# A 4-output convolution form with pixels kept apart by four, and softmax sums spread by way of DRAM

## The chip, the core and the metric

The kernel runs on one core of one Trainium2 chip. The metric is the time of the kernel on the device, in microseconds. Everything is computed in fp32. TensorE (PE) multiplies, VectorE (DVE) and ScalarE (ACT) work on tiles of 128 partitions, GpSimd (POOL) and SyncE (SP) issue most DMAs. TensorE's results land in banks of [128, 512] fp32, of which the program has eight.

## What is computed

`x` has 4 images of 256 channels and 64x64 pixels. It goes through four layers. Each is added to its input, and each reads its input group-normalised (`_gn`).

```
x = x + L0(_gn(x))
# L0: xs = relu(group_norm(conv3x3(x)))
#     f = einsum('bnc,bcm->bnm', theta(xs), phi(xs));  attn = softmax(f, -1)    # 4096 x 4096 an image
#     y = einsum('bnm,bmc->bnc', attn, g(xs));  return group_norm(conv1x1(y)) * 0.1 + xs
x = x + L1(_gn(x))   # linear attention: 4 heads of 32, softmax of q and of k, rmsnorm before and after
x = x + L2(_gn(x))   # depthwise 3x3 and 1x1 convolutions, both kernels generated from the image
x = x + L3(_gn(x))   # 1x1 convolution, mixed from four experts
```

## The kernel before

Channels lie in two halves (`NH`) of 128 partitions; an image's half is 4096 elements a partition. `xp` holds the image with a border, `big` what a layer makes of it, `tpg` theta, phi and g. `tt` (L118) and `stt` (L121) stand for VectorE's two tensor operations, so many rows of the profile carry these two lines. Tiles `k4` (1024 elements) come from ten buffers, `k2` (512) from six, filters `u` from four.

**Attention.** `attend(b)` does 128 steps an image: 8 blocks of 512 queries (`q`) by 16 blocks of keys (`m`). A step issues the two logits matmuls of the next step (`pf`, L655), each followed by ScalarE's exp into `pr` (L656), then two matmuls of this step into `py` (L694). VectorE adds `pr` to `tot`. After the sixteenth step, `ended(q)` runs alongside the next steps, one part a step: `inv` is the sum of tot's halves (L663), `pss` a matmul with ones that puts each query's sum on all partitions (L667), `inv` its reciprocal (L669), `yt = py * inv`, the 1x1 convolution `ps_wy` (L678) and ScalarE's copies to `wt`. The counts beside them (`guard`) are for a test on the range of values.

**Interleaving.** All is issued in the program's order, engine by engine (`manual_schedule`). While image b attends, a `Chain` runs beside it: the rest of the layers of image b-1 (`tail`), then the convolution of image b+1 (`convolve`). Each `yield n` of the chain adds n times its rate to a credit, and each whole credit lets one attention step out. A lower yield or a lower rate puts more of the chain between two steps. `w.later(n, f)` runs f n steps on.

**Convolution.** It is done with Winograd tiles, 4 output rows of 6 input rows, and 2 output columns of 4 input columns. For each of six transformed rows, `down` makes `ra` from the normalised image; for each of four transformed columns, `across` makes `v` (one VectorE operation of 1024 elements); `products` (L403) does two matmuls of 512 columns for each half of the outputs, with filters loaded from DRAM; `joined` adds the products to even and odd columns, `joining` and `rows_joined` join the rows into `image`, a view of `big`. Image 0 (`convolve_first`) has nothing beside it and does part of its rows with plain 3x3 products. `filter_across` works the filters out at the start and stores them in DRAM. `normalise` does half on VectorE (L474) and half on ScalarE (L476). `normed_relu` (L492) does eight ScalarE operations of 1024 and after each a DMA that adds the result to a copy of x in DRAM.

**Tail.** Layer 1 has chunks `qkv` (L784), then `outputs`, `scaled`, `added` for eight chunks of 512 pixels: `ps_o` (four matmuls of 256 columns, L852), squares on ScalarE (L854), `zr` by VectorE (L856) and POOL (L210), `z` by VectorE, transposes `ps_zt` (L875), a scaled addition and statistics (L877). Layer 2 starts with `hidden` (`ps_h`, L929) beside eight ScalarE operations that write `xp` (L942). The last image's tail runs after all attention.

Of the kernel before, what the change touches and what calls it, by code (L numbers as in the profile page):

```python
# [34 lines left out]
TY, MY, TX, MX = 6, 4, 4, 2  # L35
IY, IX = HW // MY, HW // MX

# [53 lines left out]
def conv_preact_fast(ctx: ExitStack, tc: tile.TileContext, guard, x, wc, wtpg, ww, wqkv, wout, w1cat, wd2,  # L91
# [11 lines left out]
    def k4(name):  # L103
        return wk.tile([P, CH], F32, tag="k4", name=name, bufs=10)
# [3 lines left out]
    def k2(name):  # L108
        return wk.tile([P, 512], F32, tag="k2", name=name, bufs=6)
# [18 lines left out]
    big = cp.tile([P, NH, N], F32, name="big")  # L128
    tpg = cp.tile([P, 3, N], F32, name="tpg")
    ra = cp.tile([P, NH, IY, HW + 2], F32, name="ra")  # L130
    rt = cp.tile([P, NH, IY, HW], F32, name="rt")
# [24 lines left out]
    bigf = big.rearrange("p h n -> p (h n)")  # L156
# [79 lines left out]
    filters = tc.dram_tile([TY, NH, P, TX, NH, P], F32, name="filters")  # L236
# [30 lines left out]
    def filter_across(a, stay=False):  # L267
# [4 lines left out]
        if stay:  # L272
            both = [k2("both_u").rearrange("p (h o) -> p h o", h=NH) for _ in range(2)]
        else:
            t = k4("both_u").rearrange("p (b h o) -> p b h o", b=2, h=NH)
            both = [t[:, b] for b in range(2)]
# [8 lines left out]
        for oh in range(NH):  # L285
            for k in range(TX):
                nc.sync.dma_start(out=filters[a, oh, :, k], in_=of(k)[:, :, bass.ts(oh, P)])
        return lambda k, oh, h: of(k)[:, h, bass.ts(oh, P)]

# [60 lines left out]
    def rows_of(k, h=None):  # L350

        sel = slice(k, k + MY * (IY - 1) + 1, MY)
        return xp[:, :, sel, :] if h is None else xp[:, h, sel, :]
# [4 lines left out]
    def down(a, to, prior=None):  # L358

        A, T = inside(to), rt  # L360
        mul, add, sub = ALU.mult, ALU.add, ALU.subtract
        if a in (0, 5):
# [9 lines left out]
        return [(stt, A[:, h], T[:, h], -2.0 if a == 2 else -4.0, inside(prior)[:, h], mul, add) for h in range(NH)]  # L372

    def across(k, rows):

        def col(j):
            return rows[:, :, :, j:j + MX * (IX - 1) + 1:MX]
# [3 lines left out]
        tt(v.rearrange("p (h y x) -> p h y x", h=NH, x=IX), col(first), col(second), op)  # L381
        return v

    ACROSS = (1, 2, 0, 3)

    def joiner(st):

        dst, one = [None] * NH, [None] * NH

        def stats(k):  # L390
            for oh in range(NH):
                for s in range(2):
                    nc.vector.bn_stats(st[:, oh, 2 * k + s, :], image[:, oh, bass.ts(s, IY // 2), k, :])
# [1392 lines left out]
```

## Time and profile before

| | |
|---|---|
| median of three runs | 3144.88 us (3144.27 to 3146.38) |
| profiled execution | 3145.76 us, its span 3144.0 us |
| granted TensorE clock, mean | 0.987 |
| VectorE, ScalarE, GpSimd busy | 66%, 36%, 4% of the span |
| chain that ended last | PE 80%, DVE 12%, issue 5%, ACT 2% |
| bytes read and written in HBM | 103.40 and 73.40 MB |

A group's row reads: line, engine, operation, output and inputs, shapes, count, then busy time in all and mean ns of one, then the engine's idle time just before and what ended it. An fp32 matmul appears as two records; records overlap, so what matmuls cost is read from where the next begins. In a timeline, the first number is the start and the second the length; what stands in brackets is the idle time before it.

```profile
PE   6899999999999999999999999999999999996888
DVE  8736766443547995877536896778363768855485
ACT  2233224332555332323364432222445443333510
```

These are the busy tenths of 40 equal slices: VectorE is densest where a convolution or layer 2's depthwise part runs beside attention.

### The profile page before, as it was taken

To read this page: it belongs to the slowest core of one execution; us is meant where nothing else is said; L and a number is where in the kernel's file an instruction comes from. 1 tells how busy PE (TensorE), PEld (TensorE's weight loads), DVE (VectorE), ACT (ScalarE), POOL (GpSimd) and SP (SyncE) were. 2 spreads that over 40 slices of the span, in tenths; PEclk is the share of its full clock that TensorE was granted. 3 is DMA by queue.
4 is the path that set the end of the run, shared out by engine and by line. 5 is a ranking of instruction groups with operands and counts; after the bars stand their busy time and mean duration, and the time that the engine had idled before them with its cause. 6 is when DMAs were issued, how large, how long until landed. Compare 5 with 4: busy or idle time off the path is not lost.

```text
span 3144.0 us, 24213 instructions
## 1 busy us (share of the span) xinstructions
PE 3033.0 (96%) x8526; PEld 1472.9 (47%) x8526; DVE 2079.6 (66%) x2611; ACT 1129.2 (36%) x2097; POOL 131.6 (4%) x175
## 2 busy tenths in 40 slices
PE   6899999999999999999999999999999999996888
PEld 3454444445564444444565444444545544443533
DVE  8736766443547995877536896778363768855485
ACT  2233224332555332323364432222445443333510
POOL 0000000000010000000011000000100100000100
PEclk9999999999999999999999999999999999998999
DMA  5610013001100023113300102310410010120011
GB/s 184 182 34 26 32 35 66 7 14 47 67 11 21 20 74 116 39 39 67 114 8 3 41 20 77 110 44 31 113 62 1 11 34 14 47 74 34 14 60 65
DMA packets 73985, 161.68 MB, mean 51 GB/s; under 512 B 7936, under 2 KB 39424, under 8 KB 70912
## 3 DMA queue, kind: packets, MB, share of 16 engines
q1 hardware_dynamic: 69248, 143.27, 13.3%
q0 software_dynamic: 4608, 16.78, 2.9%
q8 instruction: 70, 1.15, 0.2%
q14 instruction: 59, 0.48, 0.0%
HBM read 103.40 MB, written 73.40 MB: 56 GB/s over the span
## 4 chain that ended last, share of the span: by engine, by line
PE 80%; DVE 12%; issue 5%; ACT 2%; DMA 0%; POOL 0%; SPq 0%; POOLq 0%; ACTq 0%
PE pf L655 23%; PE py L694 23%; PE ps_conv L403 8%; PE ps_qkv L784 5%; DVE dw L121 4%; PE ps_tp L631 4%; PE ps_ex L1117 3%; PE ps_pw L979 3%; DVE tot L118 2%; PE ps_g L636 2%; PE ps_wy L678 2%; PE ps_o L852 1%; PE ps_ctx L806 1%; PE ps_dw L1014 1%; PE ps_ss L770 1%
## 5 line engine op out<-in xcount | busy, mean ns | idle before, releaser
L656 ACT ACTIVATE pr<-pf 128x512 f32<-128x512 f32 x1024 | 604.2, 596 | 1227.3 <-PE pf L655 1214.2
L655 PE MATMUL pf<-tpg 128*128 128x512 f32 x2048 | 967.2, 595 | 1.4 <-ACT pr L656 1.4
L694 PE MATMUL py<-pr,tpg 128*128 128x512 f32 x2048 | 962.1, 592 | 3.0 <-ACT pr L656 2.9
L118 DVE TENSOR_TENSOR tot<-tot,pr 128x1024 f32<-128x1024 f32 x448 | 546.3, 1219 | 249.7 <-ACT pr L656 248.1
L694 PEld LDWEIGHTS py<-pr,tpg 128*128 128x128 f32 x2048 | 388.8, 190 | 494.3 <-issue 479.8
L655 PEld LDWEIGHTS pf<-tpg 128*128 128x128 f32 x2048 | 381.5, 190 | 443.0 <-issue 419.1
L121 DVE SCALAR_TENSOR_TENSOR dw<-xp,dk,dw 128x1008 f32<-128x1008 f32 x216 | 272.9, 1267 | 6.8 <-ACT dw L971 3.7
L403 PE MATMUL ps_conv<-v,u 128*128 128x512 f32 x576 | 259.0, 596 | 3.6 <-DVE v L118 3.6
L403 PEld LDWEIGHTS ps_conv<-v,u 128*128 128x128 f32 x576 | 109.7, 191 | 143.5 <-issue 136.6
L784 PE MATMUL ps_qkv<-wqkv_s,xg 128*128 128x384 f32 x384 | 129.9, 487 | 0.0
L631 PE MATMUL ps_tp<-big,wtpg_s 128*128 128x512 f32 x256 | 118.0, 605 | 3.0 <-ACT big L492 3.0
L118 DVE TENSOR_TENSOR tpg<-ps_g,bg_s 128x512 f32<-128x512 f32 x32 | 22.1, 691 | 145.6 <-PE ps_g L636 145.6
L210 POOL TENSOR_TENSOR rstd<-rstd,half 128x2 f32<-128x2 f32 x24 | 16.8, 700 | 2419.3 <-DVE rstd L315 2225.7
L979 PE MATMUL ps_pw<-dw,pk 128*128 128x512 f32 x224 | 104.6, 601 | 8.1 <-DVE dw L121 8.1
L669 DVE RECIPROCAL inv<-pss 128x512 f32<-128x512 f32 x32 | 107.3, 3352 | 7.2 <-PE pss L667 7.2
L784 PEld LDWEIGHTS ps_qkv<-wqkv_s,xg 128*128 128x128 f32 x384 | 72.2, 190 | 53.6 <-issue 9.6
L794 DVE TENSOR_REDUCE qs<-qk 128x16 f32<-128x512 f32 x24 | 16.5, 686 | 119.0 <-ACT qk L788 119.0
L118 DVE TENSOR_TENSOR v<-ra 128x1024 f32<-128x1024 f32 x72 | 86.7, 1219 | 0.4
L632 ACT ACTIVATE tpg<-ps_tp,btp_s 128x512 f32<-128x512 f32 x64 | 43.9, 687 | 119.6 <-PE ps_tp L631 119.6
L631 PEld LDWEIGHTS ps_tp<-big,wtpg_s 128*128 128x128 f32 x256 | 47.9, 195 | 55.0 <-issue 50.6
L854 ACT ACTIVATE junk<-ps_o 128x256 f32<-128x256 f32 x128 | 49.2, 384 | 67.5 <-PE ps_o L852 59.4
L979 PEld LDWEIGHTS ps_pw<-dw,pk 128*128 128x128 f32 x224 | 43.0, 192 | 62.6 <-issue 51.9
(281 smaller groups left out, 2904.6 us busy)
## 6 DMA issues: line engine op xcount, KB each, us to landing
u<-filters SPq DMA_DIRECT2D x144, 128.0 KB, 2.3
xp<-in_x_dram SPq DMA_DIRECT2D x16, 1024.0 KB, 6.3
xs_d<-big POOLq DMA_DIRECT2D x32, 512.0 KB, 11.7
wy_d<-wt SPq DMA_DIRECT2D x32, 512.0 KB, 3.0
out_dram<-res SPq DMA_DIRECT2D x64, 256.0 KB, 2.0
wy<-wy_d SPq DMA_DIRECT2D x28, 512.0 KB, 5.2
xs<-xs_d SPq DMA_DIRECT2D x24, 512.0 KB, 5.3
wp<-in_wp_dram SPq DMA_DIRECT2D x16, 512.0 KB, 4.6
```

What stands on the lines that cost most here:

```text
L118: nc.vector.tensor_tensor(o, a, b, op)
L121: nc.vector.scalar_tensor_tensor(o, a, s, b, op0, op1)
L403: nc.tensor.matmul(ps[oh], u(oh, h), v[:, bass.ts(h, 512)], start=(h == 0), stop=(h == NH - 1))
L631: nc.tensor.matmul(ps, wtpg_s[:, h, k, :], big[:, h, cols], start=(h == 0), stop=(h == NH - 1))
L636: nc.tensor.matmul(ps[:, j, :], big[:, h, bass.ts(4 * c + j, P)], wtpg_s[:, h, 2, :], start=(h == 0), stop=(h == NH - 1))
L655: nc.tensor.matmul(pf, phi[:, bass.ts(2 * m + s, P)], theta[:, bass.ts(q, 512)], start=True, stop=True)
L656: nc.scalar.activation(pr[:, bass.ts(s, 512)], pf, AF.Exp)
L669: nc.vector.reciprocal(inv, pss)
L694: nc.tensor.matmul(py, g[:, bass.ts(2 * m + s, P)], probs[i][:, bass.ts(s, 512)], start=(m == 0 and s == 0), stop=(m == NM - 1 and s == 1))
L784: nc.tensor.matmul(ps[:, 0:3 * HID], xg[:, h, bass.ts(j, P)], wqkv_s[:, h, :], start=(h == 0), stop=(h == NH - 1))
L979: nc.tensor.matmul(ps, pk[:, h * NH * P + oh * P:h * NH * P + (oh + 1) * P], dw[h][:, bass.ts(s, 512)], start=(h == 0), stop=(h == NH - 1))
L1117: nc.tensor.matmul(ps, wm[h][:, bass.ts(oh, P)], big[:, h, cols], start=(h == 0), stop=(h == NH - 1))
```

## The change

Images 1 to 3 are convolved with 6 transformed columns that give 4 output columns, as the rows already did; image 0 keeps the old form, under names that end in `_first`. The normalised image is written into `big`, rearranged so that pixels 0, 4, 8 ... of a row stand side by side, then 1, 5, 9 ... and so on, each of the four runs with one pixel of border: rows of 68 elements (`planar`). `ra` and `rt` have such rows too, and the outputs lie in `outs`, a view of `xp`, in the same manner, as 16-element runs. Six columns are done as three pairs. `across` fills a `v` of two columns with four, three or four operations, `products` does eight matmuls of 256 columns into two banks, and `joined` makes sums and differences of a pair (`parts`), which are put into the four output columns when the second pair is there. `normed_relu` brings the pixels back in order in 16 ScalarE operations of 512 elements, and adds to DRAM in four pieces of 1 MB instead of eight of 512 KB. `normalise` puts six of its eight operations on ScalarE; it also clears the borders on GpSimd.

The filters of these images are made during the attention of image 0 (`filters_across`), from rows stored in DRAM (`rows_d`); at the start, only image 0's own are made. A load of filters is 256 KB, into three buffers in place of four of 128 KB. `k4` has nine buffers, `k2` five.

For 31 of the 32 blocks of queries, `ended` lets four matmuls with one column of ones put the sums on partitions, [128, 4], takes 512 reciprocals there, writes them to DRAM (`inv_d`) and reads them back to all partitions; two more steps of attention pass before `yt`.

Yields fall: `qkv` 0.125 to 0.04, layer 1's chunks before it 0.5 to 0.2, `outputs` twice 0.6 to twice 0.2, `hidden` 0.5 to 0.15, the mixing of experts 0.5 to 0.25. The rate for image 0's attention falls from 1.5 to 1.34; for images 1 and 2 it is 0.83 in the tail and 0.7 in the convolution instead of 0.86, and for image 3's attention 1.46 instead of 1.24.

```diff
-TY, MY, TX, MX = 6, 4, 4, 2
+TY, MY, TX, MX = 6, 4, 6, 4
 IY, IX = HW // MY, HW // MX
+TX1, MX1 = 4, 2
+IX1 = HW // MX1
+RW = MX * (IX + 1)
...
-        return wk.tile([P, CH], F32, tag="k4", name=name, bufs=10)
+        return wk.tile([P, CH], F32, tag="k4", name=name, bufs=9)
...
-        return wk.tile([P, 512], F32, tag="k2", name=name, bufs=6)
+        return wk.tile([P, 512], F32, tag="k2", name=name, bufs=5)
+    def filter_tile(name):
+        return wk.tile([P, NH, NH * P], F32, tag="u", name=name, bufs=3)
...
-    big = cp.tile([P, NH, N], F32, name="big")
+    big_all = cp.tile([P, NH, (HW + 2) * RW], F32, name="big")
+    big = big_all[:, :, 0:N]
     tpg = cp.tile([P, 3, N], F32, name="tpg")
-    ra = cp.tile([P, NH, IY, HW + 2], F32, name="ra")
-    rt = cp.tile([P, NH, IY, HW], F32, name="rt")
+    ra = cp.tile([P, NH, IY, RW], F32, name="ra")
+    rt = cp.tile([P, NH, IY, RW], F32, name="rt")
...
+    rows_d = tc.dram_tile([TY, P, NH, 3, NH * P], F32, name="rows_d")
+    filters = tc.dram_tile([TY, P, TX - 2, NH, NH * P], F32, name="filters")
...
+    def keep(rows):
+        for a in rows:
+            nc.sync.dma_start(out=rows_d[a], in_=u1[:, a].rearrange("p h (j o) -> p h j o", j=3))
...
+    def filters_across(w):
+        n = NH * 3 * NH * P
+        def load(a):
+            t = big[:, a % 2, 0:n].rearrange("p (h j o) -> p h j o", h=NH, j=3)
+            nc.sync.dma_start(out=t, in_=rows_d[a])
+            return t
+        loaded = [load(0), load(1)]
+        yield 2
+        for a in range(TY):
+            t = loaded[a]
+            f = big[:, a % 2, n:n + (TX - 2) * NH * NH * P].rearrange("p (k h o) -> p k h o", k=TX - 2, h=NH)
+            first, mid, last = (t[:, :, j, :] for j in range(3))
+            for op, *args in ((tt, f[:, 0], first, last, ALU.add), (tt, f[:, 1], f[:, 0], mid, ALU.subtract),
+                              (tt, f[:, 0], f[:, 0], mid, ALU.add), (stt, f[:, 2], last, 4.0, first, ALU.mult, ALU.add),
+                              (stt, f[:, 3], mid, -2.0, f[:, 2], ALU.mult, ALU.add),
+                              (stt, f[:, 2], mid, 2.0, f[:, 2], ALU.mult, ALU.add)):
+                op(*args)
+                yield 0.3
+            if a + 2 < TY:
+                loaded.append(load(a + 2))
+            nc.sync.dma_start(out=filters[a], in_=f)
...
+    planar = big_all.rearrange("p h (y x) -> p h y x", x=RW)
+    PIXEL = (50, 0, 17, 34, 51, 1)
+    outs = x_cols.rearrange("p h (j k n) -> p h k j n", j=MX, k=MY)
+    rt_outs = rt.rearrange("p h y x -> p h (y x)")[:, :, 0:N // MY].rearrange("p h (j n) -> p h j n", j=MX)
...
+    PAIRS = ((1, 2), (3, 4), (0, 5))
+    def across(pair):
+        v = k4("v").rearrange("p (k n) -> p k n", k=2)
+        mul, add, sub = ALU.mult, ALU.add, ALU.subtract
+        rows = ra.rearrange("p h y x -> p (h y) x")
+        def col(j):
+            return rows[:, :, PIXEL[j]:PIXEL[j] + IX]
+        def cols(j):
+            return rows[:, :, PIXEL[j]:PIXEL[j] + 2 * (IX + 1)].rearrange("p r (k i) -> p k r i", k=2)[:, :, :, 0:IX]
+        vt = v.rearrange("p k (r i) -> p k r i", i=IX)
+        one, two = v[:, 0], v[:, 1]
+        def each(j, f, *other):
+            return [(stt, vt[:, i], col(j + i), f, other[i], mul, add) for i in range(2)]
+        ops = {0: lambda: each(2, -5.0, col(4), col(5)) + each(0, 4.0, vt[:, 0], vt[:, 1]),
+               1: lambda: each(1, -4.0, col(3), col(4)) + [(tt, one, one, two, add), (stt, two, two, 2.0, one, mul, sub)],
+               3: lambda: [(tt, vt, cols(3), cols(1), sub), (stt, one, one, 2.0, two, mul, add),
+                           (stt, two, two, 2.0, one, mul, sub)]}
+        return v, ops[pair[0]]()
...
+        def products(pair, v, u):
+            banks = []
+            for i in range(2):
+                ps = bank("ps_conv")
+                for oh in range(NH):
+                    for h in range(NH):
+                        nc.tensor.matmul(ps[:, bass.ts(oh, IY * IX)], u[i][:, h, bass.ts(oh, P)],
+                                         v[:, i, bass.ts(h, IY * IX)], start=(h == 0), stop=(h == NH - 1))
+                banks.append(ps)
+            if pair != (0, 5):
+                parts[pair] = k4("sums").rearrange("p (k n) -> p k n", k=2)
+                nc.scalar.mul(parts[pair][:, 0], banks[0], -1 / 6 if pair == (1, 2) else 1 / 24)
+            return banks
+        def joined(a, pair, ps, end):
+            def put(*terms):
+                to = outs[:, :, a] if a < 4 else rt_outs
+                for j, f, t, other in terms:
+                    t, other = (None if z is None else z.rearrange("p (h n) -> p h n", h=NH) for z in (t, other))
+                    o = to[:, :, j]
+                    stt(o, t, f, o if other is None else other, ALU.mult, ALU.add)
+            if pair == (0, 5):
+                put((0, 0.25, ps[0], None), (3, 1.0, ps[1], None))
+            elif not end:
+                s = parts[pair]
+                f = -1 / 6 if pair == (1, 2) else 1 / 24
+                stt(s[:, 1], ps[1], -f, s[:, 0], ALU.mult, ALU.add)
+                stt(s[:, 0], ps[1], f, s[:, 0], ALU.mult, ALU.add)
+            else:
+                near, far = parts[1, 2], parts[3, 4]
+                put(*((j, f, far[:, j % 2], near[:, j % 2]) for j, f in enumerate((1.0, 2.0, 4.0, 8.0))))
+            return [outs[:, oh, a] if a < 4 else rt_outs[:, oh] for oh in range(NH)]
...
+        nb = negated(gm, rstd)
+        for t in (planar[:, :, 0, :], planar[:, :, HW + 1, :],
+                  planar.rearrange("p h y (r i) -> p (h y) r i", r=MX)[:, :, :, IX:IX + 1]):
+            nc.gpsimd.memset(t, 0.0)
+        for q in range(4):
+            for h in range(NH):
+                rows = slice(q * HW // 4, (q + 1) * HW // 4)
+                src = xin[:, h, rows, :].rearrange("p y (i r) -> p y r i", r=MX)
+                to = planar[:, h, rows.start + 1:rows.stop + 1, :].rearrange("p y (r i) -> p y r i", r=MX)[:, :, :, 0:IX]
+                if h == 0 and q < 2:
+                    nc.vector.tensor_scalar(to, src, gm[:, 0:1], rstd[:, 0:1], ALU.subtract, ALU.mult)
+                else:
+                    nc.scalar.activation(to, src, AF.Identity, bias=nb[:, h:h + 1], scale=rstd[:, h:h + 1])
+            yield 0.5
...
+        if b > 0:
+            for s in range(2):
+                tiles = bass.ts(s, IY // 2)
+                for h in range(NH):
+                    for k in range(MY):
+                        nc.scalar.activation(
+                            image[:, h, tiles, k, :].rearrange("p i (t j) -> p i j t", j=MX),
+                            outs[:, h, k].rearrange("p j (i t) -> p i j t", t=IX)[:, tiles], AF.Relu,
+                            bias=sh[:, h:h + 1], scale=sc[:, h:h + 1])
+                        yield 0.15
+                    cols = bass.ts(s, N // 2)
+                    w.later(1, lambda h=h, cols=cols: add_by_dma(xs_d[b, h, :, cols], big[:, h, cols]))
+            return
...
+            a, pair = PRODUCTS[i]
             res = []
-            for oh in range(NH):
-                u = wk.tile([P, NH, P], F32, tag="u", name="u", bufs=4)
-                nc.sync.dma_start(out=u, in_=filters[PRODUCTS[i][0], oh, :, PRODUCTS[i][1]])
+            for k in pair:
+                u = filter_tile("u")
+                nc.sync.dma_start(out=u, in_=rows_d[a, :, :, 0 if k == 0 else 2] if k in (0, 5) else filters[a, :, k - 1])
                 res.append(u)
-            return lambda oh, h: res[oh][:, h, :]
+            return res
...
+        for i, (a, pair) in enumerate(PRODUCTS):
+            if pair == PAIRS[0]:
+                for op, *args in down(a, planar, ra, rt, ra):
                     op(*args)
-                    yield 0.35
-            v, u = across(k, ra), us
+                    yield 0.75
+            (v, ops), u = across(pair), us
             if i + 1 < len(PRODUCTS):
                 us = load_filters(i + 1)
-            w.later(1, lambda a=a, k=k, v=v, u=u: multiply(a, k, v, u))
-            yield 0.8
+            for op, *args in ops:
+                op(*args)
+                yield 0.4
+            w.later(1, lambda a=a, pair=pair, v=v, u=u: multiply(a, pair, v, u))
+            yield 1
...
-            nc.vector.scalar_tensor_tensor(inv, tot[:, 0:512], 1.0, tot[:, 512:CH], ALU.mult, ALU.add,
-                                           accum_out=guard[:, 0, at:at + 1])
-            yield
-            pss = bank("pss")
-            nc.tensor.matmul(pss, ones, inv, start=True, stop=True)
-            yield
-            nc.vector.reciprocal(inv, pss)
+            if b == B - 1 and q == NQ - 1:
+                nc.vector.scalar_tensor_tensor(inv, tot[:, 0:512], 1.0, tot[:, 512:CH], ALU.mult, ALU.add,
+                                               accum_out=guard[:, 0, at:at + 1])
+                yield
+                pss = bank("pss")
+                nc.tensor.matmul(pss, ones, inv, start=True, stop=True)
+                yield
+                nc.vector.reciprocal(inv, pss)
+                nc.scalar.activation(junk(), inv, AF.Copy, accum_out=guard[:, 1, at:at + 1])
+            else:
+                few = [t.rearrange("p (q j) -> p j q", j=4) for t in (tot[:, 0:512], tot[:, 512:CH])]
+                sums = inv.rearrange("p (j q) -> p j q", j=4)
+                nc.vector.scalar_tensor_tensor(sums, few[0], 1.0, few[1], ALU.mult, ALU.add, accum_out=guard[:, 0, at:at + 1])
+                yield
+                pss = bank("pss")
+                for j in range(4):
+                    nc.tensor.matmul(pss[:, j:j + 1], sums[:, j, :], ones[:, 0:1], start=True, stop=True)
+                r = sp.tile([P, 4], F32, name="rsum")
+                nc.vector.reciprocal(r, pss[:, 0:4])
+                nc.vector.tensor_reduce(guard[:, 1, at:at + 1], r, AX.X, ALU.add)
+                yield
+                nc.sync.dma_start(out=inv_d[b, q].rearrange("(p j) -> p j", j=4), in_=r)
+                inv = wk.tile([P, 512], F32, tag="inv", name="inv2")
+                nc.sync.dma_start(out=inv, in_=inv_d[b, q].partition_broadcast(P))
+                yield
+                yield
             yt = k2("yt")
             tt(yt, py, inv, ALU.mult)
             yield
-            nc.scalar.activation(junk(), inv, AF.Copy, accum_out=guard[:, 1, at:at + 1])
...
+    def at(rate, part):
+        def layers(w):
+            w.rate = rate
+            yield from part(w)
+        return layers
...
-            parts = [tail(b - 1, big, qT)] if b > 0 else [scale_weights]
+            parts = [at(0.83, tail(b - 1, big, qT))] if b > 0 else [at(1.34, both(scale_weights, filters_across))]
             if b == 0:
                 load_x(1)
-            run(Chain(both(*parts, lambda w: convolve(w, b + 1)), 1.5 if b == 0 else 0.86).steps(), attention)
+            parts.append(at(1.34 if b == 0 else 0.7, lambda w: convolve(w, b + 1)))
+            run(Chain(both(*parts)).steps(), attention)
...
-        run(Chain(tail(B - 2, big, qT, held=held), 1.24).steps(), attention)
+        run(Chain(tail(B - 2, big, qT, held=held), 1.46).steps(), attention)
```

## The prediction

> **What bounds the kernel now.** I read the busy times first, then what TensorE waits for, then the stretches that the change touches, and the groups for prices.
>
> ```profile
> PE 3033.0 (96%) x8526; PEld 1472.9 (47%) x8526; DVE 2079.6 (66%) x2611; ACT 1129.2 (36%) x2097; POOL 131.6 (4%) x175
> ```
>
> ```profile
> 0.00:150.00 150.00, 117.80 (x269) 0.97 0.54 183
> 150.00:2800.00 2650.00, 2631.43 (x7357) 1.00 0.15 44
> 2800.00:3144.00 344.00, 283.72 (x902) 0.90 0.14 48
> ```
>
> The second view gives length, TensorE's busy time and its clock. TensorE bounds the kernel: of 111 us that it is idle, 32 lie in the first 150 us and 60 after 2800. The change keeps TensorE's order in both places. The middle 2650 us hold only 18.6 us of idle time. So in the middle any TensorE time taken away is gained, and any wait added is lost: no slack takes it up.
>
> ```profile
> PE ps_zt L875 <- DVE z L118: 5.4, 8, 1.1
> PE ps_conv L403 <- DVE v L118: 3.6, 2, 1.9
> PE py L694 <- ACT pr L656: 2.9, 2, 1.4
> ```
>
> These waits of TensorE (total, count, longest) mark the places where the middle is thin: attention waits for ScalarE's exp (py), the convolution for VectorE (ps_conv), layer 1's outputs for z.
>
> ```profile
> L403 PE MATMUL ps_conv<-v,u 128*128 128x512 f32 x576 | 259.0, 596 | 3.6 <-DVE v L118 3.6
> L118 DVE TENSOR_TENSOR v<-ra 128x1024 f32<-128x1024 f32 x72 | 86.7, 1219 | 0.4
> L669 DVE RECIPROCAL inv<-pss 128x512 f32<-128x512 f32 x32 | 107.3, 3352 | 7.2 <-PE pss L667 7.2
> L492 ACT ACTIVATE big<-big,sh,sc 128x1024 f32<-128x1024 f32 x32 | 37.4, 1232 | 36.3 <-DVE sh L118 36.3
> L760 ACT ACTIVATE xg<-big,nb,rstd 128x512 f32<-128x512 f32 x48 | 36.4, 807 | 7.5 <-DVE nb L118 7.5
> L942 ACT ACTIVATE xp<-big,nb,rstd 128x1024 f32<-128x1024 f32 x24 | 28.8, 1235 | 0.0
> ```
>
> [...] eight records of 512 take 3.43 us (next start less own start, ps_conv at 1308.75 to 1312.18), eight ps_o records of 256 take 1.73 (964.41 to 966.14), half. [...] the trace has 691 (yt). [...] the trace has 807. Splitting work into smaller instructions therefore costs VectorE and ScalarE, not TensorE. [...]
>
> **Part 1, convolution on TensorE (gain).** Before: 3 images x 24 products, each eight records of 512: 72 x 3.43 = 247.0 us. After: 3 x 18 pairs x 2 groups of eight records of 256: 108 x 1.73 = 186.8. Gain 60.2. Image 0 is unchanged.
>
> **Part 2, softmax sums (gain).** 31 of 32 sums become four one-column matmuls; eight one-column records (ps_ss, 2916.45 to 2917.26) take 0.81 us, the old pss 0.85: 1.2 us gained. VectorE loses 31 x 3.35 = 103.9 us of reciprocals.
>
> **Part 3, VectorE's convolution work.** Per image, across: 24 x 1.22 = 29.3 before; after, six rows of ten 512-element steps and one of 1024, 6 x (10 x 0.69 + 1.22) = 48.7. Joins: 6 x 8 x 0.68 = 32.7 before, 6 x 10 x 0.70 = 42 after. Rows of 68 instead of 64 pixels add some 2, and two normalise steps fewer give 1.6. So +29 an image, +87 in all; filters_across adds 36 x 0.69 = 24.8 and takes 8.3 out of image 0's convolution. The total is as before (-103.9 + 87 + 16.5); but the convolution's stretches are denser. In 1055 to 1480, VectorE is busy 344.8 of 425 us (81%). After, about 345 + 29 - 15 (four or five reciprocals) over 405: 89%. A running sum of both engines' durations in program order puts VectorE's backlog at 9 to 13 us at its peaks, against 7 to 13 before, with products placed about as late. Bounds for TensorE's waits: 0 to 10 over three images. I take 3.
>
> **Part 4, ScalarE's bursts (loss).** Attention can run one step (3.43 us) ahead of its exp. Before, the relu steps stand 2, 4 and 2 between pairs of exp, and the four cost a wait:
>
> ```profile
> 1467.04 4.63 ACT L492 ACTIVATE big<-big,sh,sc 128x1024 f32<-128x1024 f32 x4
> 1472.20 1.98 PE L694 MATMUL py<-pr,tpg 128*128 128x512 f32 x4 [1.44 <-ACT pr L656]
> ```
>
> After, 16 of 512 elements replace 8 of 1024, with yields that put ten, an exp pair, then six for images 2 and 3. At 0.72 us back to back (an estimate from the 807 row, less the overlap that ScalarE shows between neighbours) ten take 7.2, or 2.6 to 3 more than four of the old: waits of 4.4 and 2.0 instead of 1.44, +5.0 each. Image 1 (4, 5, 5, 2): +2.4. Six instead of four normalise steps on ScalarE: +1 for images 2 and 3. Sum 14.4.
>
> **Part 5, layer 1's outputs (loss).** Yields of 0.2 instead of 0.6 leave three chunks of ps_o and ps_zt between attention steps where there was about one on each side of one. A chunk's VectorE work is two z (0.68), two scaled sums (0.74) and two statistics (0.69), with zr: about 4.6 us with its waits; its TensorE work is 1.73 + 0.87 = 2.6. The ending shows the stage with little attention beside it:
>
> ```profile
> 2956.77 0.87 PE L875 MATMUL ps_zt<-ident,z 128*128 128x128 f32 x6 [1.06 <-DVE z L118]
> 2967.61 1.44 PE L875 MATMUL ps_zt<-ident,z 128*128 128x128 f32 x6 [1.00 <-DVE z L118]
> 2978.45 0.88 PE L875 MATMUL ps_zt<-ident,z 128*128 128x128 f32 x6 [1.00 <-DVE z L118]
> ```
>
> 4.6 - 2.6 leaves about 1.9 us a chunk, of which four a tail are uncovered: 7 for tails 0 and 1. Tail 2 keeps a step at every one or two chunks: 4. Sum 18. Bounds: 5 (the buffers of z let TensorE run ahead) to 25.
>
> **Part 6, hidden stage and qkv (loss).** With 0.15 for 0.5, six xp steps of 1.13 follow each other on ScalarE, where before each two had an exp pair behind them. 6.8 us less the step ahead (3.43) and slack already used makes +2.9 for tails 0 and 1, +1.5 for tail 2; pm and pv close together +1 each, which is 9 with rounding up. qkv chunks at 0.04: 0 to 4, I take 1.
>
> **Part 7, the round trip of the sums.** Inverse sums now go out (nearest rows: rw_s 1 KB 2.1 us, wy_d 3.0) and come back to all partitions (bo_s, 128 KB to all, 3.0): 5.2 to 7 us after the sums. yt stands on VectorE 5.8 to 9 us behind the sums in the running sum, ps_wy on TensorE 13.7 to 20.7. yt is a wait in order: behind it on VectorE stand tot, v and joins, and pr's buffers wait for tot. In five cases a load of u stands ahead on SP's queue and waits for a product 8.6 to 12.1 us behind the sums. SP's queue already carries such waits, which cost little now:
>
> ```profile
> SPq L540 <- PE ps_conv L403: 510.2, 132, 32.3
> ```
>
> Those five land at about 17 us, within ps_wy's cover or just past it. Bounds 0 to 6.5; I take 2. The ScalarE pass over inv that counted its sum (31 x 0.63) goes; it was hidden.
>
> **Neutral.** Filters: rows_d and filters are written and read in larger pieces off the path, under attention. POOL's memsets lie in an engine 4% busy. About 3 of the old 18.6 us of waits go with the stages that they stood in.
>
> **Sum.** -61.4 + 14.4 + 18 + 9 + 1 + 3 + 2 - 3 = -17 us against the profiled execution's 3145.76 (span 3144.0 and 1.8 around it): 3128.8. The median shown is 0.9 lower: 3128.
>
> **Rivals.**
> 1. Full gain. The bursts fall where exp is ahead and VectorE, freed of 3.35 us blocks, keeps z on time: the parts 4 to 6 cost a quarter, 10: 3144.9 - 61.4 + 10 = 3093. For it: before, whole stretches have no wait at all. Against: the one burst of four already shows 1.44.
> 2. VectorE binds in the convolution. The new forms read and write runs of 16 elements, which no row here shows; if they take 25% longer, on about 122 us an image (across, joins, down) that is 30 more, and 89% becomes 96%: nearly each burst is a wait, some 9 an image: 3128 + 27 = 3155, slower. It decides from about 15% on. Against: z, copies and old joins with strides of two pixels cost the contiguous price (683).
> 3. The round trip is late. At 10 us and more, yt holds VectorE 1 to 4 us at each of 31 sums, and with half of it reaching TensorE, 31 x 1.1 = 34: 3162, slower. Point of decision: landing 9 us behind the sums. Against: the rows of 2 to 3 us for each DMA. For: SP's order, and completion before the read.
>
> **How the numbers follow.** Forecast 0.50 (own range 3110 to 3146), full gain 0.22, VectorE 0.14, round trip 0.12, anything else 0.02. Range 3088 to 3160: it cuts the ends of both sides. A measurement tells 0.2% (6.3 us) from no change. Faster: 0.50 x 0.82 + 0.22 + a little = 0.65; same: 0.50 x 0.15 + 0.14 x 0.4 + a little = 0.15; slower 0.20.
>
> **What would show it.** Right: ps_conv x864 of 256 columns near 187 us by starts; PE busy near 2972; waits py <- pr of 12 us or more; ps_zt <- z of 15 or more. Wrong: those waits absent (rival 1); ps_conv <- v or joins over 900 ns for 512 elements (2); ps_wy <- yt with 31 entries or yt <- inv2 over 50 us on VectorE with TensorE idle behind (3).

## The result, and the profile after

The changed kernel takes 3242.71 us (median of four runs, 3231.21 to 3251.54) against 3144.62 before: 1.0309 times as long, 95% interval 1.0267 to 1.035. The profiled execution took 3250.85, its span 3249.1. The forecast was 3128, with 3088 to 3160 as its range: wrong in sign and outside the range. Two of the four runs lie near 3233 and two near 3251, where the kernel before spreads over 2 us; what fits this is said below, with the clock.

The page's first part, of the kernel after:

```profile
PE 3028.4 (93%) x9000; PEld 1564.2 (48%) x9000; DVE 2088.1 (64%) x2822; ACT 1157.8 (36%) x2061; POOL 112.4 (3%) x172
```

TensorE is as busy as before (3033.0), though the convolution has lost a quarter of its work. Its busy time by stretch, of the kernel after (start and end, length, TensorE's busy time, clock, share of DMA, GB/s):

```profile
0.00:150.00 150.00, 115.52 (x266) 0.98 0.37 141
150.00:2800.00 2650.00, 2526.55 (x7579) 0.98 0.18 54
2800.00:3249.00 449.00, 386.37 (x1159) 0.93 0.15 53
```

In the middle TensorE is now idle for 123 us of 2650 (18.6 before), and its clock has fallen from 1.00 to 0.98. One image shows all of it: the stretch from one `project` to the next, image 2's convolution within it, first of the kernel before, then of the one after (start and end, length, then busy time and count of PE, PEld, DVE, ACT and POOL, then clock, share of DMA and GB/s).

```profile
738.38:1479.17 740.79, 733.28 (x2089) 356.50 (x2087) 525.93 (x658) 277.17 (x513) 33.08 (x39) 1.00 0.16 50
```

```profile
739.97:1525.29 785.32, 737.05 (x2233) 388.80 (x2232) 531.15 (x718) 288.94 (x507) 26.61 (x38) 0.97 0.18 56
```

The stretch is 44.5 us longer: 40.8 us more idle (48.3 against 7.5), and 3.8 more busy, although ps_conv falls from 82.5 to 65.2 us when each record is counted up to the start of the next ("by its starts"). The attention matmuls alone, the same 1024 in both, take 443.0 before and 459.0 after by their starts. So the 17.3 us saved are spent on running the rest at a lower clock, and the idle time is the loss. Images 2 and 3 have the same stretch twice (89 us); the stretch for image 1 is as long as before (591 and 592), and what follows image 3's project is 15 us longer.

What TensorE waits for, of the kernel after (total, times, longest):

```profile
PE py L860 <- ACT pr L803: 49.5, 15, 7.7
PE pm L336 <- DVE mv L124: 42.0, 8, 20.5
PE pm L336 <- DVE mv L331: 22.7, 3, 17.0
PE ps_zt L1041 <- DVE z L124: 21.0, 13, 2.4
PE ps_conv L475 <- DVE v L124: 12.2, 5, 3.9
...
PE ps_conv L475 <- DVE v L127: 6.5, 2, 3.3
...
PE ps_wy L844 <- DVE yt L124: 6.4, 5, 2.3
```

The first row was 2.9 us before. (Of pm's two rows, 18.8 us lie in the middle 2650 us; the longest waits, 20.5 and 17.0, stand outside it and stood there before.) By what ScalarE did just before, 26.5 of the 49.5 us stand behind relu, 17.1 behind normalise and 6.0 behind the operations of layer 2's hidden stage. The reason is in the groups of the kernel after:

```profile
L475 PE MATMUL ps_conv<-v,u 128*128 128x256 f32 x864 | 203.4, 389 | 21.4 <-DVE v L124 12.2 <-DVE v L127 6.5 <-issue 2.7
L617 ACT ACTIVATE big<-xp,sh,sc 128x512 f32<-128x512 f32 x48 | 52.6, 1265 | 10.6 <-DVE sh L124 10.6
L127 DVE SCALAR_TENSOR_TENSOR v<-ra 128x512 f32<-128x512 f32 x72 | 47.4, 683 | 0.1
L590 ACT ACTIVATE big<-xp,nb,rstd 128x1024 f32<-128x1024 f32 x18 | 39.2, 2241 | 9.8 <-DVE nb L127 9.8
```

Relu takes 1265 ns for 512 elements, where an operation of this size with two operands took 807 before, and normalise 2241 for 1024, where it took 1232. Both step over pixels four apart: relu where it writes, normalise where it reads. VectorE's forms with 16-element runs (683, v<-ra) cost what a contiguous one of 512 costs (688, v<-v).

The timeline of the end of image 2's convolution, after, ScalarE then TensorE:

```profile
1499.68 10.78 ACT L617 ACTIVATE big<-xp,sh,sc 128x512 f32<-128x512 f32 x10 [3.84 <-DVE sh L124]
1510.27 1.09 ACT L803 ACTIVATE pr<-pf 128x512 f32<-128x512 f32 x2
```

```profile
1501.34 1.88 PE L802 MATMUL pf<-tpg 128*128 128x512 f32 x4
1510.94 3.49 PE L860 MATMUL py<-pr,tpg 128*128 128x512 f32 x4 [7.72 <-ACT pr L803]
1514.27 1.88 PE L802 MATMUL pf<-tpg 128*128 128x512 f32 x4
```

Ten relus hold the exp back, and TensorE is idle for 7.72 us. Then the next four records take 3.49 us instead of 1.88: the gap is paid a second time, at half a clock. The granted clock in this trace is either full or half, and in the middle 2650 us a stretch at half clock is 3.41 us (14 of them) or 6.83 us long (10), so it costs 1.7 us or twice that where TensorE has work. Summed over slices of 10 us of the middle 2650 us, one less the clock comes to 2.6 us in the kernel before, and to 58.8 after; some 8 of the 58.8 fall into TensorE's own idle time and lengthen nothing.

In each of the 14 traces, all stretches at half clock start on one grid of 3.413 us (in the changed kernel's, all 32 within 0.02 us of it). A piece of this grid is called a window here. In the middle 2650 us, the 14 traces have 154 windows at full clock in which TensorE was idle for 60% or more (matmuls of under 64 columns counted as idle), 22 of them in the changed kernel's: each was followed by a window at half clock. Of 10371 that were idle for less than half, none was; of 72 between, 18 were. So some 2 us of idle time within one window (60% of 3.413) were enough here, and what a gap of 2 to 4 us costs depends on where it lies on the grid. One wait of 2.63 us shows both, in the changed kernel and in the run called no_rearrangement below:

```profile
985.83 1.98 PE L860 MATMUL py<-pr,tpg 128*128 128x512 f32 x4 [2.63 <-ACT pr L803]
```

```profile
972.59 2.54 PE L861 MATMUL py<-pr,tpg 128*128 128x512 f32 x4 [2.63 <-ACT pr L804]
974.92 3.07 PE L803 MATMUL pf<-tpg 128*128 128x512 f32 x4
```

Here are the window of the grid that holds most of this wait and the one after it, first of the changed kernel, then of no_rearrangement (start and end, length, TensorE's busy time and count, clock; the last two numbers are DMA). Idle for 1.75 us of 3.41, the clock stays; idle for 2.12, it is halved.

```profile
981.53:984.94 3.41, 1.66 (x4) 1.00 0.00 0
984.94:988.35 3.41, 2.52 (x6) 1.00 0.00 0
```

```profile
970.47:973.88 3.41, 1.29 (x3) 1.00 0.00 0
973.89:977.30 3.41, 3.41 (x5) 0.50 0.00 0
```

Counted from the span's start, the grid's lines lie at 1.59 us in the trace of the kernel before, at 1.90 in the changed kernel's and at 1.08 in no_rearrangement's (each plus multiples of 3.413). If the grid also lies differently in each execution of one kernel, its gaps cost more in one than in another. That fits the wider spread of the changed kernel's runs; it isn't shown for them.

### The profile page after: what moved, and what is told of

It is laid out like the page before. It is cut to its first block, busy times and chain, and to the rows that moved or that the text cites. A ratio compares the mean times of both kernels' runs of the same rounds, so it can differ in the third digit from the quotient of the medians.

```text
span 3249.1 us, 25336 instructions
## 1 busy us (share of the span) xinstructions
PE 3028.4 (93%) x9000; PEld 1564.2 (48%) x9000; DVE 2088.1 (64%) x2822; ACT 1157.8 (36%) x2061; POOL 112.4 (3%) x172
## 5 line engine op out<-in xcount | busy, mean ns | idle before, releaser
L860 PE MATMUL py<-pr,tpg 128*128 128x512 f32 x2048 | 978.8, 601 | 49.5 <-ACT pr L803 49.5
L802 PE MATMUL pf<-tpg 128*128 128x512 f32 x2048 | 986.8, 605 | 0.1
L124 DVE TENSOR_TENSOR tot<-tot,pr 128x1024 f32<-128x1024 f32 x448 | 546.3, 1219 | 189.1 <-ACT pr L803 188.0
L802 PEld LDWEIGHTS pf<-tpg 128*128 128x128 f32 x2048 | 389.1, 194 | 434.1 <-issue 416.4
L127 DVE SCALAR_TENSOR_TENSOR dw<-xp,dk,dw 128x1008 f32<-128x1008 f32 x216 | 273.0, 1267 | 13.6 <-ACT dw L1137 10.9
L475 PE MATMUL ps_conv<-v,u 128*128 128x256 f32 x864 | 203.4, 389 | 21.4 <-DVE v L124 12.2
L475 PEld LDWEIGHTS ps_conv<-v,u 128*128 128x128 f32 x864 | 167.2, 195 | 69.1 <-issue 22.5
L127 DVE SCALAR_TENSOR_TENSOR sums<-ps_conv,sums 128x512 f32<-128x512 f32 x72 | 49.6, 688 | 52.1 <-PE ps_conv L475 46.6
```

The costliest lines, as they stand in the source:

```text
L124: nc.vector.tensor_tensor(o, a, b, op)
L127: nc.vector.scalar_tensor_tensor(o, a, s, b, op0, op1)
L475: nc.tensor.matmul(ps[:, bass.ts(oh, IY * IX)], u[i][:, h, bass.ts(oh, P)], v[:, i, bass.ts(h, IY * IX)], start=(h == 0), stop=(h == NH - 1))
L802: nc.tensor.matmul(pf, phi[:, bass.ts(2 * m + s, P)], theta[:, bass.ts(q, 512)], start=True, stop=True)
L860: nc.tensor.matmul(py, g[:, bass.ts(2 * m + s, P)], probs[i][:, bass.ts(s, 512)], start=(m == 0 and s == 0), stop=(m == NM - 1 and s == 1))
```

## The experiments

The theories are named by letters in the expectations. S: the loss is in ScalarE's and VectorE's dense stretches, each longer gap then lengthened by the clock. R: the round trip of the sums. Y, B, C, K and L are told where they occur. In the code cuts, "..." marks lines left out. The numbers in brackets are the ratio to the kernel before and its 95% interval.

**The sums as before**, in the changed kernel:

```diff
-            if b == B - 1 and q == NQ - 1:
...
-                nc.sync.dma_start(out=inv, in_=inv_d[b, q].partition_broadcast(P))
+            nc.tensor.matmul(pss, ones, inv, start=True, stop=True)
+            yield
+            nc.vector.reciprocal(inv, pss)
```

> The changed kernel with the softmax sums of the kernel before (reciprocal of 128x512, nothing by way of DRAM). Theory S (ScalarE's strided forms in dense bursts, late VectorE in the convolution, and half a clock after each longer gap of TensorE): the relu and normalise waits stay (py <- pr near 45 us), only the five held yt (42.6 us on VectorE, 6 us of TensorE's ps_wy waits) go, while the reciprocals bring 104 us back to VectorE: 3225 to 3255 us. Theory R (the round trip of the sums through DRAM holds VectorE and so everything): 3200 us or less, and the convolution's waits for v fall by half.

3232.03 us (1.0274, 1.0257 to 1.0291): its interval and the changed kernel's overlap. py <- pr stays at 45.3. The trip is not the cause of most of the loss.

**The sums by way of DRAM alone**, in the kernel before.

> The kernel before with only the new softmax sums (four one-column matmuls, small reciprocal, through DRAM and back). Theory S: little or nothing, 3140 to 3155 us. Theory R: holds of yt on VectorE of some 40 us or more, and 3165 us or more.

3158.98 us (1.0048, 1.0031 to 1.0065): a loss of about 15 us, between the two theories. The trace, of the fastest of the four executions, has one held yt (7.8 us), 8.5 us more span, and a clock sum of 7.1 us instead of 2.6. So this part of the change loses by itself. In this one hold it is the trip that is long: the write of the sums took 8.1 us to land (515.86 to 523.96).

**The yields as before**, with the tail's number of steps kept:

```diff
-                yield 0.04
+                yield 0.125
...
-            yield 0.2
+            yield 0.6
...
-            parts = [at(0.83, tail(b - 1, big, qT))] if b > 0 else [at(1.34, both(scale_weights, filters_across))]
+            parts = [at(0.695, tail(b - 1, big, qT))] if b > 0 else [at(1.34, both(scale_weights, filters_across))]
```

> The changed kernel with the yields of the kernel before in qkv, layer 1's chunks, outputs, hidden and the mixing of experts, the tail's rate lowered from 0.83 to 0.695 (1.46 to 1.23) so that the tail gets as many attention steps as in the changed kernel, but spread as before. Theory S: ps_zt <- z falls from 21 us to 6, the waits in the hidden stage (10.6 us) go, with about eight slow stretches of 1.7 us behind them: 30 to 40 us less, 3200 to 3215 us; the relu and normalise waits stay. Theory Y (the thinned tail is most of the loss): 3170 us or less. Theory R: no more than 10 us less.

3218.0 us (1.0237, 1.022 to 1.0255). That is 25 us less, where S had 30 to 40, and far from Y. ps_zt <- z falls from 21.0 to 8.5 us (6 was expected), but ps_pw <- dw rises from 8.1 to 15.7 and ps_wy <- yt from 6.4 to 10.5: steps given to one stage are missed in another.

**The other order of pixels** on ScalarE:

```diff
-                            image[:, h, tiles, k, :].rearrange("p i (t j) -> p i j t", j=MX),
-                            outs[:, h, k].rearrange("p j (i t) -> p i j t", t=IX)[:, tiles], AF.Relu,
+                            image[:, h, tiles, k, :].rearrange("p i (t j) -> p i t j", j=MX),
+                            outs[:, h, k].rearrange("p j (i t) -> p i t j", t=IX)[:, tiles], AF.Relu,
```

> The changed kernel, with ScalarE's relu and normalise walking the pixels in the other order, so that the stride of pixels lies on the other operand (relu writes side by side and reads with a stride of 16 elements; normalise reads side by side and writes with a stride of 17). Theory S1 (a stride on either side costs ScalarE double): relu stays near 1.26 us, normalise near 2.24, time within 15 us of 3243. Theory S2 (only a stride of four pixels on the side that it is on now costs): relu 0.81, normalise 1.24, and the waits of py for pr fall by 30 us or more, to about 3190 us with the clock.

3242.09 us (1.0302, 1.0285 to 1.0319); relu 1267 ns, normalise 2121. S1 holds: with the stride on the other operand, relu costs 1.6 times and normalise 1.7 times what it costs without (803 and 1234 ns in the next run).

**No rearrangement** on ScalarE: relu and normalise read and write neighbours. This kernel leaves the rearrangement out, so that images 1 to 3 hold their pixels in another order and its output is not the program's.

> The changed kernel, but ScalarE's relu and normalise write runs of neighbouring elements where they read such runs: the rearrangement of pixels on ScalarE is left out (images 1 to 3 hold their pixels in another order), sizes and counts stay. Theory S (the stride of four pixels doubles ScalarE's time in its bursts): relu falls from 1.27 to 0.81 us, normalise from 2.24 to 1.23, the waits of py for pr from 49 us to about 18, with some of the slow clock behind them: 3195 to 3212 us. Theory B (the density of the bursts is enough to cause them): 3230 us or more.

3198.69 us (1.0169, 1.0155 to 1.0183): 44 us less, with the same counts, sizes and steps. The groups of this run:

```profile
L618 ACT ACTIVATE big<-xp,sh,sc 128x512 f32<-128x512 f32 x48 | 34.7, 803 | 10.7 <-DVE sh L124 10.7
L591 ACT ACTIVATE big<-xp,nb,rstd 128x1024 f32<-128x1024 f32 x18 | 21.1, 1234 | 7.4 <-DVE nb L127 7.4
```

py <- pr falls to 17.8 us (9.9 behind relu, 2.0 behind normalise, 6.0 in the hidden stage), the clock sum from 58.8 to 27.8. The stride itself is shown as the cause of 44 us by the medians. The two profiled spans differ by 55 us: 32 of waits for pr, and 22 less busy time of TensorE, which has the same matmuls at a higher clock. The wait behind ten relus is 4.15 us now:

```profile
1482.51 3.64 PE L861 MATMUL py<-pr,tpg 128*128 128x512 f32 x4 [4.15 <-ACT pr L804]
```

**Useless matmuls in the gaps**, for images 2 and 3:

```diff
+    def filler(n):
+        ps = bank("fill")
+        for _ in range(n):
+            nc.tensor.matmul(ps, ww_s[:, 0:P], tpg[:, 0, 0:512], start=True, stop=True)
...
+                        if b > 1 and s + h + k == 0:
+                            filler(8)
```

> The changed kernel with useless matmuls (128x128 by 128x512, never read) for images 2 and 3 at four places where TensorE waits: three before the input's pm (wait 2.83 us), six in normalise (5.7), five before the convolution's pm (4.99), eight in relu (7.7). 44 matmuls, 37.8 us of TensorE. Theory K (idle gaps of TensorE bring half a clock for 3.4 us after): the slow stretches behind these places go, about 9.7 us an image, and the work itself falls into the waits: 3215 to 3230 us. Theory L (the lower clock doesn't come from the gaps): 3243 or, with what doesn't fit into the waits, up to 3260 us, and the clock as it was.

3239.46 us (1.03, 1.0286 to 1.0314): not told apart from the changed kernel. The slow stretches behind the two waits for pm and behind normalise are gone, and the clock sum is 34.5 us instead of 58.8; but 37.8 us of matmuls took away only 33 us of waits, and at relu the wait moved on. TensorE's timeline of this run:

```profile
1492.71 7.11 PE L571 MATMUL fill<-tpg,ww_s 128*128 128x512 f32 x16
...
1505.90 1.98 PE L874 MATMUL py<-pr,tpg 128*128 128x512 f32 x4 [0.93 <-ACT pr L817]
1507.72 1.88 PE L816 MATMUL pf<-tpg 128*128 128x512 f32 x4
1513.29 3.78 PE L874 MATMUL py<-pr,tpg 128*128 128x512 f32 x4 [3.68 <-ACT pr L817]
```

The filled gap is followed by full speed, the one that is left by half: in favour of K where the gap was filled. The time lies between the two theories' ranges, so as a sum of time it stays inconclusive.

**The bursts spread** over more steps, taken from the convolution:

```diff
-                        yield 0.15
+                        yield 0.45
...
-            yield 0.5
+                yield 0.6
...
-                yield 0.4
+                yield 0.36
```

> The changed kernel with attention steps moved from between the convolution's products to between its relu and normalise operations: yields 0.15 to 0.45 at relu, 0.5 each quarter to 0.6 each operation at normalise, in the convolution 0.4 to 0.36 and 1 to 0.9, the rate in image 0's attention 1.34 to 1.31. Theory S: py <- pr falls from 49 us to 15 or less, the convolution's waits for v grow by less than 10: 3200 to 3220 us. Theory C (VectorE limits the convolution's stretch, so that steps taken from it are lost there): 3235 us or more.

3191.24 us (1.0162, 1.0145 to 1.0179): 51 us less, below what was expected, and C falls. py <- pr is 14.9 us, though relu still takes 1297 ns. So the stride hurt where many strided operations stood together with few steps between them. This and no_rearrangement (44 us) take away largely the same waits, and their savings don't add up.

**Three parts undone**: yields, sums, rearrangement (left out as above, with the output in another order).

> The changed kernel with the yields of the kernel before, its softmax sums, and the rearrangement of pixels on ScalarE left out (as in no_rearrangement): the 4-output convolution on TensorE and VectorE stays. Theory S: what is left is the convolution's own waits; 3150 to 3175 us. Theory C (the convolution's stretch itself, dense on VectorE, gives back more than the 60 us that it saves): 3185 us or more, with waits for v, sums and pm as they were.

3187.25 us (1.013, 1.0115 to 1.0146), as C had it in size but not in place: v's waits are small (7.2), while ps_pw <- dw has grown to 24.6 us and ps_wy <- yt to 13.1. The old yields at the rate of 0.695 seem to leave too few steps to layer 2, as in yields_as_before (15.7); that is a reading of the waits and wasn't tried alone.

**Steps by need.** A stage needs (its time on VectorE or ScalarE, less its own time on TensorE) over what a step leaves of that engine: 3.43 - 1.22 = 2.2 us on VectorE, about as much on ScalarE. Relu: 19.4 us of ScalarE an image, so 8 to 9 steps; it had 3. In the same way normalise gets 4 with half of it on VectorE (it had 1.4), layer 1's outputs 5 (2.7), and the convolution 33 (44).

```diff
-                        yield 0.15
+                        yield 0.66
...
-                if h == 0 and q < 2:
+                if h == 0:
...
-            yield 0.5
+            yield 1.5
...
-                    yield 0.75
+                    yield 0.58
...
-                yield 0.4
+                yield 0.3
...
-            yield 0.2
+            yield 0.4
```

> The changed kernel with attention steps given to each stage by what its VectorE or ScalarE work lacks in TensorE work (worked out from the rows: relu 19.4 us of ScalarE an image, so 8 steps in place of 3; normalise 4 in place of 1.4, half of it on VectorE; outputs 5 in place of 2.7; the convolution 33 in place of 44). Theory S (the loss is where the steps lie: work on ScalarE and VectorE in stretches without enough TensorE work, each gap then lengthened by the clock): py <- pr under 8 us, ps_zt <- z under 16, v's waits under 25, 3150 to 3170 us. Theory C (the convolution needs its 44 steps): waits for v and sums over 45 us, no better than bursts_spread's 3191.

3142.97 us (0.9996, 0.9989 to 1.0003): 100 us less than the changed kernel, with the same instructions but for two normalise operations an image that go to VectorE, and a little below what S had. py <- pr has gone to 0.8 us, and C falls again. Waits of TensorE in this run:

```profile
PE ps_zt L1041 <- DVE z L124: 13.0, 11, 2.6
PE ps_conv L475 <- issue: 9.7, 4, 3.8
...
PE ps_conv L475 <- DVE v L124: 6.2, 1, 6.2
```

**The same with the old sums**, and **with the sums' DMAs issued by GpSimd**:

```diff
-                nc.sync.dma_start(out=inv_d[b, q].rearrange("(p j) -> p j", j=4), in_=r)
+                nc.gpsimd.dma_start(out=inv_d[b, q].rearrange("(p j) -> p j", j=4), in_=r)
...
-                nc.sync.dma_start(out=inv, in_=inv_d[b, q].partition_broadcast(P))
+                nc.gpsimd.dma_start(out=inv, in_=inv_d[b, q].partition_broadcast(P))
```

> As respread, with the softmax sums of the kernel before (reciprocal of 128x512 on VectorE). The round trip cost 10 us in the changed kernel and 14 alone; the reciprocals cost VectorE 27 us an image where the convolution has fewer steps now. Theory S: within 12 us of respread, on either side. Theory R: 10 us or more below it.

> As respread, with the two DMAs of the softmax sums issued by GpSimd, whose queue holds no load that waits for a product. If SP's order makes the five holds of yt, they go (yt <- inv under 8 us on VectorE against some 40) and ps_wy <- yt with them: 6 to 12 us below respread. If the trip's own length does it: the same or above, with more holds.

3136.59 us (0.9975, 0.9964 to 0.9986) and 3135.18 (0.9965, 0.995 to 0.9979). Both are below both kernels, 8 and 9 us below the one before. The two lie 1.4 us apart: without its holds, the new form of the sums is worth hardly more than the old one. What VectorE waits for at yt, first in respread, then with GpSimd's DMAs:

```profile
DVE yt L124 <- DMA inv<-inv_d: 43.7, 7, 11.3
```

```profile
DVE yt L124 <- DMA inv<-inv_d: 2.9, 3, 1.1
```

So in this kernel the holds came from SP's order, where a load of filters waits for a product ahead of them, and not from the length of the trip. SP's queue shows it before the hold that ends at 470.75 in the changed kernel: the load (L682) had waited for a product, the sums' write (L832) could only follow it, and the read (L834) is issued when the write has landed (466.73); so are all 31 reads of this trace, 0.02 to 0.14 us after their write's landing. All five holds there stand so, with the write 0.4 to 0.6 us behind a load that waited for ps_conv.

```profile
464.07 0.32 SPq L682 DMA_DIRECT2D u<-filters  x1
464.44 0.42 SPq L832 DMA_DIRECT2D inv_d<-rsum  x1
466.74 0.32 SPq L834 DMA_DIRECT2D inv<-inv_d  x1
```

**The convolution's end eased**, after that: three units before its last pm (8.25 us there), taken from relu and the tail.

> As respread_gpsimd_sums, with three more units (2.1 attention steps) between the convolution's last statistics on VectorE and the pm that waits for them (8.25 us in images 2 and 3), taken from relu (0.66 to 0.58) and the tail (rate 0.83 to 0.815; 1.36 to 1.33 in image 0's attention). Theory S (steps where VectorE is behind): pm's wait there falls to 2 us or less and the slow stretch after it with it, py and z waits grow by less than 5 in all: 3110 to 3127 us. Theory C (the convolution's backlog only shows up elsewhere): 3130 us or more.

3145.28 us (1.0005, 0.9996 to 1.0013): C. pm's wait falls only to 5.8 us, the steps are missed elsewhere (py <- pr rises from 0.8 to 6.4 us, ps_wy <- yt from 0.7 to 5.4), and an image's stretch grows from 741 to some 749.5 us.

## Why the prediction was wrong

The frame held: TensorE bounds the kernel, the middle has no slack, and each wait added there counts. By its parts:

- Part 1 was right. By starts, ps_conv falls by 54.7 us over three images (17.3 in image 2's), where 60.2 was forecast; part of it runs at half clock now.
- Part 2 and part 7 had the size of the sums wrong: a loss of about 1 us together, and about 15 when measured alone. Its five held loads are the five holds of yt in the trace (42.6 us on VectorE), and the trip's length was right (6.3 us from the write's issue at 464.44 to the landing at 470.73). That the five land just in time was the error: ps_wy waited 6.4 us. Part 2 also left out that the sum of tot's halves now reads with a stride of four, which costs VectorE 12 us in all; first the group before, then after:

```profile
L663 DVE SCALAR_TENSOR_TENSOR inv<-tot 128x512 f32<-128x512 f32 x32 | 22.1, 692 | 1.1
```

```profile
L823 DVE SCALAR_TENSOR_TENSOR inv<-tot 128x512 f32<-128x512 f32 x31 | 33.7, 1087 | 1.1
```

- Part 3 is a term that was too small: 3 us for the convolution's waits; those for v rose by 15.1 us (from 3.6 to 18.7), and those of pm by 14.5. Their bound of 10 was too low. The slow forms that rival 2 asked of VectorE in the convolution were not there (683 ns).
- **Part 4 failed first.** It priced relu at 0.72 us back to back from a contiguous row, and normalise at +1 for an image. The trace has 1.06 back to back (ten in 10.78 us) and 2.24 for a normalise operation. Ten relus are so 10.8 us and not 7.2. TensorE's waits for pr behind relu and normalise rose by 40.6 us (43.5 against 2.9), where 14.4 was forecast; normalise alone has 17.1, where 2 was forecast. Without the stride, in no_rearrangement, they rise by 9.0, and the wait behind ten relus is 4.15, where part 4 had 4.4: the bursts were placed rightly and their operations priced wrongly. The text doubted the form for VectorE and took it as given for ScalarE. What it is in ScalarE that makes the stride cost isn't shown.
- Parts 5 and 6 were right in size: ps_zt <- z rose by 15.6 us (18), and the hidden stage shows 10.6 us in two images (9), half of it waits for pr.
- **A term was missing.** No part has the clock. Of its 58.8 us after, less 2.6 before and the 8 that fall into idle time, some 48 lengthen the work, nearly what the convolution gained. It shows in TensorE's busy time, 3028.4 us, where the prediction had 2972. The middle of the kernel before had shown no price for it, since it had almost no gaps; only its ending did (0.90, with 60 us idle).

With part 4 at its measured size (26 more), part 3 with 15.1 for v (12 more) and 14.5 for pm, and 48 for the clock, the sum of the forecast (-17) becomes -17 + 26 + 12 + 14.5 + 48 = 83.5; the profiled executions differ by 105, the medians by 98. What is left, some 20 us, isn't placed term by term; smaller waits are in it, such as 4.6 us of ps_conv's for other reasons. None of the rivals named the cause. The nearest in time, the round trip, was not it.

That the steps lay wrongly for these prices is shown, since respread has the same parts, and the same fewer buffers, and takes back 100 us. What stays open is the convolution's own gain: with steps by need and GpSimd's sums, the stretches with the convolutions of images 2 and 3 are still as long as before (741 us, in an execution 7.6 us below its median), and most of what is gained comes from the stretch with image 1's, which falls from 592.3 to 574.5 us. The fewer buffers were not tried by themselves.

## What to carry to other kernels

Where one engine is filled by interleaving, the cover is a budget: count for each stage what its slower engine lacks, and give steps by that, since making a stage shorter on the bounding engine also takes away its cover. Before a layout is changed, ask each engine that crosses from old to new what a stride costs it, and price a new gap of TensorE at more than its length. An estimate, from the grid of 3.413 us and the shares of 60% and half counted above, is: a gap of over 4.1 us (twice 60% of a window) leaves one window idle for 60% and costs some 1.7 us more in the next (half of 3.41), one of under 1.7 us (half a window) alone costs nothing more, and between them it is a matter of where it falls.

## What the runs showed of the hardware

ScalarE took 1.27 us instead of 0.81 for 512 elements and 2.24 instead of 1.23 for 1024 with a stride of four fp32, written in the one and read in the other; with strides of 16 and 17 elements much the same (1.27, 2.12). On VectorE, a read stride of four fp32 took tensor_scalar from 0.81 to 1.44 us (1024 elements) and a sum of two tensors from 0.69 to 1.09 (512), while its operations in runs of 16 elements cost nothing more (0.68, against 0.69 contiguous). In the kernel before, two operations of 512 elements took longer than one of 1024: 2 x 691 against 1219 ns on VectorE, 2 x 807 against 1232 on ScalarE.

In the middle of the changed kernel, 9 of 16 gaps of TensorE between 1.8 and 2.7 us, 7 of 8 between 2.8 and 4 us and all 6 above 4 us were followed by 3.41 or 6.83 us at half a clock. So were 2 of 11 between 0.9 and 1.8 us, both of 1.3 us with tiny matmuls beside them. In all 14 traces the idle share of a window of the 3.413 us grid went with it: a window at full clock was followed by one at half clock in all 154 cases of 60% or more, and in none of 10371 of less than half. At half clock, less went with staying there: all 78 such windows that were idle for a fifth or more were followed by another, and none of the 161 that were idle for under a tenth.
